# Two cross-attention layers on one core: a packed image product, maxima taken after the second scores, a split last entry and another order of the opening

## The chip, the core and the metric

The kernel runs on one core of a Trainium2 chip. The core has a matrix engine (TensorE, PE in the profile; PEld is its loading of weights), a vector engine (VectorE, DVE), a scalar engine (ScalarE, ACT), GpSimd (POOL) and SyncE (SP), which here only issues transfers. All of them run at once and wait for each other by semaphores. PE writes its products to PSUM, eight banks of 128 x 512 fp32; data that stay on the core lie in SBUF.

The metric is the time of one execution in microseconds of the device, from its start to its end. The profile is one further execution, whose instructions were recorded.

## What is computed

There are 16 batch entries of 256 positions and 320 channels, 20 heads of 16 channels, and a context of 256 tokens of 512 channels for each entry. In layer 1 the first 77 tokens are text and the other 179 image tokens; in layer 2 the first 252 are text and the last four are image tokens. Both layers have this form (shown for layer 2; layer 1 takes its own similarity from one softmax over the channels of all heads together, and has no norms):

```python
q = heads(x @ W_q); k_t = heads(text @ W_k); v_t = heads(text @ W_v)
probs_t = softmax(q @ k_t.T * scale)
text_out = probs_t @ v_t
k_ip = heads(ip @ W_k_ip); v_ip = heads(ip @ W_v_ip)
qsem = l2norm(probs_t @ text)
sem = qsem @ l2norm(ip).T
probs_ip = softmax(q @ k_ip.T * scale + 0.5 * sem) * spatial_mask
out = (text_out + probs_ip @ v_ip) @ W_out + b_out + x
```

The second layer's `x` is the first layer's `out`. All inputs and outputs are fp32.

## The kernel before

**Precision.** A product of two fp32 tiles takes two records of PE in the profile. Most products are therefore made of halves: each tile is split into a rounded part and a remainder (`halves`, lines L187 and L188), both of type fp32r, and `prod` (L260) sums three single-pass products, high by high, high by low and low by high. The same is done in the output projection (`project`, L632). The image product of layer 2 (L1108) is one of those left in plain fp32.

**Slots.** The heads are handled in groups of four, five groups for each entry, so a layer has 80 slots (one slot is one group of one entry): 0 to 79 are layer 1, 80 to 159 layer 2. The queries and keys of a slot, its stacks, are loaded from DRAM four slots ahead (`LEAD`).

**A slot of layer 2** (`slot1`). `both1(k, t)`, once for each half t of the positions, writes the transposed scores of slot k (L917, tiles T, read by ACT's exponential L929) and the plain scores of slot k+2 (L922, tile S). S takes two banks and has a single buffer; T has two tiles, P one and X three of a bank each. DVE takes the maximum over S (L923) and copies the image scores out of it (L939). The maxima are then turned by two products with a unit matrix (`maxima1`, L955) into one row, copied by ACT (L957) and stored by a DMA on ACT's queue (L959) into row `XROW` of the query stack. There it is one more row of the contraction of L917, so that the exponentials are taken of scores less their maximum. `attend1` (L988, L990) multiplies the probabilities by the values into the lower half of a P bank; its last products, with the matrix `zone` (L990), add the sums for the norm, taken from the tiles W. `norm1` multiplies the rounded probabilities (`rounded1`: ACT rounds at L965, POOL keeps the remainder at L966) by a matrix of the context (L975, 14 products of 512 columns in a slot); DVE multiplies the result by W (L978) and the two parts are added (L980, on POOL for the first two heads and on DVE for the others). `settle1` (L1040 to L1044) turns the attended tile with a DVE transpose and divides by the sums.

**An entry of layer 2.** Beside its five slots an entry has steps spread over the slots around it: `k1` its keys (`keys1`; L564 is the remainder of the split), `t1` its values and the context matrix (`tokens1`, L585 to L602), `o1` its queries (`open1`, L615 to L618 and L640, L641), `gather` (L864, three DVE transposes of the result), `i1` the softmax over the image tokens (`image_softmax`, L1051 to L1101, most of it on POOL) and `c1` its end (`close1`): for each of three blocks of rows the image product (L1108, the table `vb` of image values, 128x384, by the turned probabilities `pT`, turned at L1100), the sum with the transposed text result (L1109, on DVE), the split (L871, L873), 24 products with the output weights and the residual (L895). The table of each entry is loaded from `spread_d` in DRAM, which `weights8` makes once at the layer change: it fills it with zeros from a tile and then copies blocks of the image values (`vipd`, stored by `weights6`) to their places.

**What sets the order.** PE's order is written by the program in all stages. In `begin`, which is the opening up to slot 0, every engine's order is; in layer 2 (slots 80 to 159) that of all engines but SP; in layer 1 and after slot 159 the other engines' order is left to the scheduler. Steps are `task`s with due times in slots (the table `STEPS`; for an entry of layer 2 relative to its first slot): at given points of each slot `fill` runs all steps that have come due. DVE instructions that are given to `late` are put off while `hold` is in force and are issued at `release`, or at the next `settled`. Nearly all DMAs are issued by SP, in order, so one that waits holds up those behind it.

**The opening.** `begin` loads the weights and the contexts of entries 0 and 1, makes keys, queries and layer 1's own similarity, and scores slots 0 and 1. The row of maxima of these two slots is stored by SP's queue (L783, behind ACT's copy L782), and the contexts of entries 2 and 3 are loaded behind that.

**The end.** The last entry, b = 15, is closed like the others, behind slots 160 and 161, which only finish the sums of slots 158 and 159.

## Time and profile before

| | us |
|---|---|
| median of 3 runs | 1479.34 |
| lowest and highest | 1478.5, 1482.8 |
| the profiled execution | 1478.29 |
| its span in the profile | 1476.5 |

The mean granted clock of PE in the profiled execution was 0.992 of full speed. The span is the time between the first and the last instruction recorded; the profiled execution's own time is 1.8 us longer.

Rows of the profile read like this: a window has its start and end, then for each engine the busy time and, in parentheses, the instructions counted, then PE's granted clock, the busy share of the DMA engines and the GB/s that they moved. A row of the timeline has the start of a group of equal instructions, the time from there to its last end, the engine, the line of the program, the operation, and output and input tiles with their sizes; in brackets the idle time before it and what ended that. A row of the chain has the start, the length and the engine with its tile and line; "issue" is time in which an engine waited for nothing that the profile shows, SPq a DMA's issue on SP, "DMA x<-y" a transfer.

### The profile page before, as it was taken

What the parts mean: (1) busy time and instruction counts of PE and PEld (TensorE: products, weight loads), DVE (VectorE), ACT (ScalarE), POOL (GpSimd) and SP (SyncE); (2) the same over time, 40 slices, a digit from 0 to 9 for tenths busy, and PEclk for the clock granted to TensorE, in tenths of its full rate; (3) what the DMA queues carried; (4) which work ended last, traced back from release to release, by engine and by line L of the source; (5) the groups of instructions that cost most, each with busy time, mean ns of one, the idle gap of its engine ahead of it and who ended that gap; (6) DMA issues with size and microseconds to landing.
All of it is one profiled execution on the core that took longest, in us unless ns stands there. A gap on an engine that the chain in (4) does not pass through costs nothing.

```text
span 1476.5 us, 35304 instructions
## 1 busy us (share of the span) xinstructions
PE 1431.7 (97%) x12438; PEld 1184.3 (80%) x12438; DVE 1167.9 (79%) x2569; ACT 955.8 (65%) x2074; POOL 1154.1 (78%) x1173
## 2 busy tenths in 40 slices
PE   6899999999999999899999999999999999999998
PEld 6788888888888878677778888888888888888865
DVE  5477776777767787977888888888888888888897
ACT  5567676767676776756666666656665666566563
POOL 5259797978787878987788878787778877887786
PEclk9899999999999999999999999999999999999999
DMA  6766666565656577665434433543454345434511
GB/s 198 170 171 178 149 158 165 152 167 147 170 151 170 149 187 215 146 184 163 135 107 140 147 117 102 161 146 102 119 161 143 93 130 160 133 100 120 150 31 50
DMA packets 230667, 211.78 MB, mean 143 GB/s; under 512 B 56314, under 2 KB 217116, under 8 KB 230492
## 3 DMA queue, kind: packets, MB, share of 16 engines
q1 hardware_dynamic: 229232, 208.57, 50.5%
q8 instruction: 99, 1.62, 0.5%
q10 hardware_dynamic: 1260, 0.97, 0.2%
q14 instruction: 76, 0.62, 0.1%
HBM read 122.07 MB, written 86.44 MB: 141 GB/s over the span
## 4 chain that ended last, share of the span: by engine, by line
PE 87%; DVE 5%; DMA 2%; ACT 2%; issue 2%; POOL 2%; SPq 1%; DVEq 0%; ACTq 0%; POOLq 0%
PE X L260 22%; PE X L975 17%; PE X L632 11%; PE P L833 7%; PE S L772 6%; PE P L988 5%; PE T L917 5%; PE T L795 5%; PE S L922 3%; PE P L990 2%; PE X L690 1%; PE X L1108 1%; POOL wt L966 1%; PE X L780 1%; SPq L83 1%
## 5 line engine op out<-in xcount | busy, mean ns | idle before, releaser
L801 POOL TENSOR_TENSOR P<-P,rs 128x512 f32<-128x512 f32 x320 | 414.4, 1319 | 142.2 <-ACT P L798 142.0
L975 PE MATMUL X<-ctb,gm 128*128 128x512 f32 x1120 | 292.2, 403 | 0.0
L966 POOL TENSOR_TENSOR wt<-P,ctb 128x512 f32<-128x512 f32 x212 | 268.5, 1295 | 0.0
L923 DVE TENSOR_REDUCE mn<-S 128x4 fp32r<-128x1008 f32 x160 | 192.8, 1205 | 80.3 <-PE S L922 78.5
L975 PEld LDWEIGHTS X<-ctb,gm 128*128 128x128 f32 x1120 | 201.2, 188 | 48.7 <-issue 0.4
L798 ACT ACTIVATE P<-T 128x512 f32<-128x512 f32 x320 | 174.7, 593 | 97.6 <-PE T L795 80.0
L978 DVE TENSOR_TENSOR wt<-X,wt 128x512 f32<-128x512 f32 x240 | 159.3, 680 | 4.0 <-PE X L975 3.4
L929 ACT ACTIVATE P<-T 128x512 f32<-128x512 f32 x212 | 115.0, 597 | 54.4 <-PE T L917 41.8
L980 POOL TENSOR_TENSOR wt<-wt 128x512 f32<-128x512 f32 x80 | 103.6, 1295 | 57.5 <-DVE wt L978 57.5
L774 DVE TENSOR_REDUCE mn<-S 128x4 fp32r<-128x716 f32 x160 | 142.4, 890 | 0.0
L965 ACT ACTIVATE ctb<-P 128x512 fp32r<-128x512 f32 x212 | 122.2, 625 | 30.4 <-PE X L975 29.2
L833 PE MATMUL P<-P,vr 128*32 128x256 f32 x1920 | 123.9, 389 | 0.6 <-DVE sp L693 0.6
L632 PE MATMUL X<-hq,wE 128*128 128x256 f32 x768 | 111.4, 290 | 4.9 <-ACT hq L615 3.6
L260 PE MATMUL X<-cta,wA 128*128 128x252 f32 (+3 forms) x726 | 104.9, 290 | 6.1 <-ACT wA L187 5.3
L632 PEld LDWEIGHTS X<-hq,wE 128*128 128x128 f32 x768 | 102.2, 196 | 7.6 <-ACT hq L615 4.0
L632 PE MATMUL X<-ho,wF 128*128 128x256 f32 x768 | 106.6, 285 | 0.9 <-DVE ho L871 0.6
L260 PEld LDWEIGHTS X<-cta,wA 128*128 128x128 f32 (+1 forms) x726 | 94.8, 191 | 10.2 <-ACT wA L187 5.6
L632 PEld LDWEIGHTS X<-ho,wF 128*128 128x128 f32 x768 | 98.7, 189 | 3.9 <-DVE ho L871 1.0
L844 DVE STREAM_TRANSPOSE nt<-P 128x512 f32<-128x512 f32 x80 | 57.1, 714 | 44.6 <-PE P L833 44.4
L833 PEld LDWEIGHTS P<-P,vr 128*32 128x32 f32 x1920 | 55.4, 111 | 41.4 <-issue 5.5
L773 DVE TENSOR_REDUCE mn<-S 128x4 fp32r<-128x308 f32 x160 | 74.4, 465 | 17.4 <-PE S L772 16.9
L917 PEld LDWEIGHTS T<-qs,ks 49*128 49x128 f32 x640 | 50.3, 184 | 46.5 <-issue 19.9
(223 smaller groups left out, 3319.6 us busy)
## 6 DMA issues: line engine op xcount, KB each, us to landing
qd<-q SPq DMA_DIRECT2D x48, 384.0 KB
kd<-kst SPq DMA_DIRECT2D x66, 256.0 KB
rawc<-in_cT_dram SPq DMA_DIRECT2D x60, 256.0 KB
qs<-qd SPq DMA_DIRECT2D x160, 96.0 KB
ks<-kd SPq DMA_DIRECT2D x160, 96.0 KB
qs<-qd SPq DMA_DIRECT2D x60, 192.0 KB
ks<-kd SPq DMA_DIRECT2D x60, 192.0 KB
qd<-q SPq DMA_DIRECT2D x32, 256.0 KB
```

Source lines behind the costliest of these rows:

```text
L260: last = mm(out, lhs(a, k), rhs(b, k), start=i == 0, stop=i == len(terms) - 1)
L632: mm(pp, w(s, k, slice(m * 128, (m + 1) * 128)), a[:, t], start=i == 0, stop=i == len(terms) - 1)
L774: anchor(nc.vector.tensor_reduce(mn[:, t, 1], sp[:, :, T0:], axis=AX.X, op=ALU.max))
L798: exp = anchor(nc.scalar.activation(pt, st[p], AF.Exp, scale=SCALE))
L801: anchor(nc.gpsimd.tensor_mul(pt, pt, rs[:, t : t + 1].to_broadcast([128, 2, S])))
L833: mm(pv[32 * s : 32 * s + 32, o : o + S], v[:, vt, h : h + 32], P[k, s // 2][:, t, s % 2], start=vt < 2, stop=vt != 1,)
L917: mm(st[u][:, j], c[1][rows, j, lo : lo + 128], c[0][rows, j], start=True, stop=True)
L923: anchor(nc.vector.tensor_reduce(maxes[k + 2][:, t], sp[:, :, :T1], axis=AX.X, op=ALU.max))
L965: nc.scalar.activation(R[k, u][:, t], P[k, u][:, t], AF.Copy, scale=0.5)
L966: anchor(nc.gpsimd.tensor_sub(W[k, u][:, t], P[k, u][:, t], f(R[k, u][:, t])))
L975: mm(yp, gm[:, gb], R[k, u][:, kt], start=i == 0, stop=i == len(blocks[n]) - 1)
L978: nc.vector.tensor_mul(product, yp, w[:, n])
```

## The change

- **Packed image product.** `vb` and `pT` are now of type fp32r. The table holds, in the 96 rows that were zero before, also the remainder of the image values: of every 32 rows 8 are used by two groups of heads, and now three times (high, high, low). The probabilities are packed beside it as high, low, high, so that one single-pass product sums all three terms. Groups 0 and 1, 2 and 3, and 4 share the three blocks, so `pT` is three tiles of 128x256 in place of one. For each entry ACT makes four small copies and three of 128x256, POOL two small subtractions, DVE three transposes in place of one. In `weights6` the image values are split (an ACT copy and a DVE subtraction) and stored with three DMAs. In `weights8` three tiles are set to zero by POOL in place of one, and the 24 copies from `vipd` move 192 pieces of 64 bytes in place of 64.
- **Maxima.** `maxima1(k + 1)` comes right behind the second `both1` of slot k and uses the upper half of the bank of `attend1`. Before, `maxima(k + 2)` came at the end of the slot with a bank of its own. `release` and, behind it, `hold` move behind the second scores, `rounded1(k, 0)` behind the third part of `norm1`, `rounded1(k, 1)` behind the stacks. `settle1` keeps its reciprocals in the lower half of the bank.
- **Split last entry.** The image softmax of entry 15 runs for groups 0 to 3 (`i1a`) and then, with DVE in POOL's place, for group 4 (`i1`). `close_first` does two thirds of the rows and of the output products early; `close_last` does the third row and six products. Residual and text result are added by fp32 products with the unit matrix. For the last slot the remainders of its second pair of heads are made on DVE, and the two parts of the norm are added by four more products with `zone`. The output goes out in three DMAs on two queues.
- **Layer change.** The due times of the weight steps stay; those of the steps of layer 2's entries (`k1`, `t1`, `o1`, `i1`, `c1`) change. The zero fill of `spread_d` is issued later on SP, just before the last stacks of layer 1 that precede `vipd`, since its source tiles come free later; all loads of `wq1` stand behind the stores of `vipd`, where the first stood in front of them before.
- **Opening.** `begin` is written out step by step. The loads of the contexts of entries 2 and 3 are issued behind the loads of the stacks of slot 2, and their keys are spread over the rest of `begin`. The row of maxima of slot 1 goes by ACT's queue. The first half of slot 0's transposed scores is made in `begin`, and `opening` takes the place of slot 0.

The order of PE is the same in both programs from about the third slot of layer 1 to shortly before the end of layer 1.

The core of the diff:

```diff
-        dma(vipd, vip)
+        high = buf("rawc", [128, 512], bufs=2, name="high")[:BI, :CP].bitcast(FR)
+        nc.scalar.copy(high, vip)
+        nc.vector.tensor_sub(vip, vip, f(high))
+        for d, v in zip(range(3), (high, high, vip)):
+            dma(vipd[d].rearrange("n b c -> (n b) c"), v)
...
-    def maxima1(k):
-        mn = maxes[k]
-        mp = bank()
+    def maxima1(k, bank):
         for t in range(2):
-            mm(mp[:4, t * 128 : (t + 1) * 128], mn[:, t], ident_r, start=True, stop=True)
+            mm(bank[:4, S + t * 128 : S + (t + 1) * 128], maxes[k][:, t], ident_r, start=True, stop=True)
         mt = buf("mt", [8, S], FR)[:4]
-        nc.scalar.copy(mt, mp[:4, :S])
+        nc.scalar.copy(mt, bank[:4, S:])
         row = QK[k][0].rearrange("(u p) j t -> u p j t", u=2)[:, XROW]
-        late(lambda: nc.scalar.dma_start(f(row), f(mt)))
+        nc.scalar.dma_start(f(row), f(mt))
...
     def slot1(k):
...
-        yield release
         yield lambda: both1(k, 1)
+        yield lambda: maxima(k + 1, summed)
         if last:
             yield lambda: norm1(last, 0, 0)
         yield 0.2
+        yield release
+        if mine:
+            yield hold
         for parts in summed:
             yield lambda: settle1(*parts)
         if last:
             yield lambda: norm1(last, 0, 1)
-        if mine:
-            yield lambda: rounded1(k, 0)
         yield 0.4
         if last:
             yield lambda: norm1(last, 1, 0)
-        yield 0.6
+        if mine:
+            yield lambda: rounded1(k, 0)
         if last:
             yield lambda: norm1(last, 1, 1)
-        if mine:
-            yield hold
+        yield 0.6
+        yield 0.8
+        yield lambda: stacks(k + LEAD)
         if mine:
             yield lambda: rounded1(k, 1)
-        yield 0.8
-        yield lambda: maxima(k + 2)
-        yield lambda: stacks(k + LEAD)
         yield 1.0
...
-        pT = w1["pT"]
-        late(lambda: nc.vector.transpose(pT, pi.rearrange("p f c -> p (f c)")))
+        for d, x in pieces:
+            (nc.vector.tensor_copy if lo else nc.scalar.copy)(d[:, :, :, :8], x)
+            nc.scalar.copy(d[:, :, :, 16:24], x)
+        yield
+        for d, x in pieces:
+            pool.tensor_sub(d[:, :, :, 8:16], x, f(d[:, :, :, :8]))
+        yield
+        turned = w1["turned"]
+        for i in turns:
+            late(lambda i=i: nc.vector.transpose(turned[i], f(packed[i // 2][:, i % 2]).rearrange("p f c -> p (f c)")))
+        yield
+        settled()
+        for i in turns:
+            nc.scalar.copy(pT[i], turned[i])
         return pT, vb
+    def close_first():
+        hT, (pT, vb) = results["gathered", B - 1, 0], get("i1a")
+        settled()
+        x, hl = load(x1d[B - 1], "xq"), buf("ho", [128, 5, S], FR)
+        def row(p):
+            hp = bank()[:, :S]
+            mm(hp, ident, hT[:, p], start=True, stop=False)
+            mm(hp, vb[:, p * 128 : (p + 1) * 128], pT[p], start=False, stop=True)
+            nc.scalar.copy(hl[:, p], hp)
+            low_half(hl, p, hp)
...
+        for m, pp in enumerate(outs):
+            mm(pp, ident, x[:, m], start=True, stop=False)
+            for s, k, t in [(s, k, t) for k in range(2) for s, t in ((0, k), (0, 3 + k), (1, k))]:
+                mm(pp, wo[1](s, k, slice(m * 128, (m + 1) * 128)), hl[:, t], start=False, stop=False)
+            yield
+    def close_last():
+        row, hl, x, outs = get("c1a")
+        get("i1", B - 1)
+        settled()
+        row(2)
+        yield
+        for m, pp in enumerate(outs):
+            for s in range(2):
+                mm(pp, wo[1](s, 2, slice(m * 128, (m + 1) * 128)), hl[:, 2], start=False, stop=s == 1)
...
+    def opening():
+        yield lambda: turned0(0, 1)
+        yield lambda: score0(2, 0)
+        yield 0.2
+        yield lambda: score0(2, 1)
+        yield lambda: stacks0(4, "QK")
+        yield 0.6
+        yield 1.0
```

227 lines of the change are left out of this document (155 added, 72 removed), and 35 rows, old and new, of the table STEPS.

## The prediction

> **What bounds the kernel now.** I read the page's busy times first, then its chain that ended last, then a table of stages, and last the timelines inside one stage.
>
> ```profile
> span 1476.5 us, 35304 instructions
> PE 1431.7 (97%) x12438; PEld 1184.3 (80%) x12438; DVE 1167.9 (79%) x2569; ACT 955.8 (65%) x2074; POOL 1154.1 (78%) x1173
> ...
> PE 87%; DVE 5%; DMA 2%; ACT 2%; issue 2%; POOL 2%; SPq 1%; DVEq 0%; ACTq 0%; POOLq 0%
> ```
>
> TensorE sets the end: 97% busy and 87% of the chain. So the change pays in two ways: fewer microseconds of products where PE has no gap, and shorter gaps where it has one. The stages tell which is where (span, then busy time and count of PE, weight loads, DVE, ACT, POOL, then clock, DMA share, GB/s):
>
> ```profile
> 55.00:60.00 5.00, 1.80 (x13) 1.24 (x11) 3.97 (x11) 2.68 (x10) 0.40 (x1) 0.91 0.39 83
> 60.00:66.00 6.00, 5.68 (x28) 5.55 (x28) 3.69 (x5) 4.07 (x10) 5.03 (x4) 0.51 0.96 280
> 66.00:71.00 5.00, 1.83 (x10) 1.26 (x8) 4.86 (x5) 1.78 (x5) 2.97 (x3) 0.83 0.54 113
> 71.00:77.00 6.00, 6.00 (x40) 4.10 (x40) 2.46 (x5) 1.29 (x3) 0.33 (x1) 0.57 0.01 3
> 990.00:1039.60 49.60, 49.60 (x420) 40.19 (x419) 42.53 (x90) 30.85 (x68) 39.47 (x44) 1.00 0.44 130
> 1388.00:1438.00 50.00, 47.70 (x370) 35.34 (x368) 45.14 (x93) 29.75 (x64) 37.92 (x43) 1.00 0.21 58
> ```
>
> Rows 1 to 4 are the opening: 22 us with 15.31 of them busy, so 6.7 idle; the clock of rows 2 and 4 costs 5.68 x 0.49 + 6.00 x 0.43 = 5.4 more. Row 5 is one batch entry of layer 2: PE busy for all of it, DVE for 86%. Row 6, the last entries: DVE for 90%.
>
> **Part 1, the packed image product.** In each layer 2 entry three fp32 products of 256 columns become single-pass products; 45 of the 48 change (the last entry's three stand in the tail, part 3). The first two rows are PE's timeline in the steady stage, the third is from the chain near the end:
>
> ```profile
> 992.84 1.02 PE L1108 MATMUL X<-rs,rs 128*128 128x256 f32 x4
> ...
> 1001.91 0.59 PE L1108 MATMUL X<-rs,rs 128*128 128x256 f32 x2
> ...
> 1443.69 1.91 PE X L632 x16
> ```
>
> Two records are one fp32 product. Two more of them lengthen the group by 1.02 - 0.59 = 0.43 us, the price of one product without its end. A single-pass product of 256 columns takes 1.91/16 = 0.12. Each saves 0.31: 0.94 an entry, 14.0 in all, if PE stays the bound.
>
> What is added for it stands on other engines: per entry ACT gets four small copies and three of 128x256, POOL two small subtractions, DVE two more transposes of 128x256. ACT was busy for 30.85 of 49.60 and POOL for 39.47: I take nothing for them, their idle 18.8 and 10.1 hide it; uncovered, ACT's three large copies, some 0.36 each by the copy of part 5, would be 1.1 an entry. DVE's two transposes are 2 x 0.44 (L1100 below), which takes it to about 43.4 of 48.7.
>
> **Part 2, the turns of the maxima.** The maxima's two products (L955) move from the slot's end to just behind its second scores (L922), into the free half of the P bank; the row that they give is wanted by the next slot's L917, in the shortest slot (below) 5.63 - 0.33 - 0.21 = 5.1 us later. Even a DMA as long as the 4.92 us load of part 5 would almost fit there and be late by ACT's work ahead of it; each microsecond of that, in the shortest slot of every entry, would be 15 us. The row has 4 KB, the load 256, and I take nothing. Deferred DVE work is let go behind the second scores, too, and what remains runs at the slot's end, ahead of the next slot's first reduction (L923). This is the point where I expect the gain to go. The same slot of before on both engines (start, busy time, idle before):
>
> ```profile
> 1029.32 0.40 PE L922 MATMUL S<-ks,qs 48*128 48x256 f32 x4
> 1029.65 2.83 PE L975 MATMUL X<-ctb,gm 128*128 128x512 f32 x11
> 1032.32 1.55 PE L260 MATMUL X<-cta,wA 128*128 128x252 f32 x12
> 1033.70 0.86 PE L975 MATMUL X<-ctb,gm 128*128 128x512 f32 x3
> 1034.40 1.92 PE L260 MATMUL X<-wC,cta 128*128 128x320 f32 x12
> 1036.16 0.28 PE L955 MATMUL X<-ident_r,mn 128*4 128x128 f32 x2
> 1036.37 0.51 PE L917 MATMUL T<-qs,ks 49*128 49x256 f32 x4
> 1036.71 0.41 PE L922 MATMUL S<-ks,qs 48*128 48x256 f32 x4
> ```
>
> ```profile
> 1029.77 1.21 DVE L923 TENSOR_REDUCE mn<-S 128x4 fp32r<-128x1008 f32 x1 [0.49 <-PE S L922]
> ...
> 1030.97 0.68 DVE L978 TENSOR_TENSOR wt<-X,wt 128x512 f32<-128x512 f32 x1
> 1031.57 0.44 DVE L1040 STREAM_TRANSPOSE nt<-P 128x256 f32<-128x256 f32 x1
> ...
> 1032.49 1.28 DVE L978 TENSOR_TENSOR wt<-X,wt 128x512 f32<-128x512 f32 x2
> 1033.69 1.09 DVE L864 STREAM_TRANSPOSE hT<-hsn 128x256 f32<-128x256 f32 x3
> 1034.70 0.38 DVE L564 TENSOR_TENSOR kst<-X,kst 128x252 fp32r<-128x252 f32 x1
> 1035.01 0.69 DVE L978 TENSOR_TENSOR X<-X,wt 128x512 f32<-128x512 f32 x1
> 1035.73 0.69 DVE L980 TENSOR_TENSOR wt<-wt,X 128x512 f32<-128x512 f32 x1
> 1036.34 0.44 DVE L1100 STREAM_TRANSPOSE rs<-rs 128x256 f32<-128x256 f32 x1
> 1037.15 1.21 DVE L923 TENSOR_REDUCE mn<-S 128x4 fp32r<-128x1008 f32 x1 [0.38 <-PE S L922]
> ```
>
> The score tile S has one buffer, so the reduction must be over before PE writes the next scores. Before, DVE waits 0.38 to 0.49 us for PE ahead of each reduction shown, and PE never for DVE. In the changed order one slot of each entry holds on PE, from its second L922 to the next slot's first, only 14 of L975 (2.67 + 0.70), 12 of L260 (1.38), L955 (0.21), L917 (0.34) and L922 itself (0.33): 4.93 + 0.70 = 5.63 us. On DVE it holds from reduction to reduction, start to start: L923 with its copy 1.20, L978 0.60, L1040 with the two behind it 0.92, two of L978 1.20, three of L864 1.01, L564 0.31, the last L978 0.72 and L980 0.61: 6.57 us. DVE comes 0.94 late. PE notices this at its second score write, which waits for that reduction; its slack there is 0.38 (by the smaller idle time; a reduction without such slack behind it would cost all 0.94). So 0.56 us of stall, where L922's wait also holds up the L975 products behind it and by them the next L978. Another slot, with L1060, L1109, L873, L587 and L618 packed ahead of the reduction, comes out near its PE time; I take 0.25, between nothing and 0.5. The other three are longer on PE and on time. Together 0.8 an entry against 0.94 saved: net -0.14, over 15 entries -2. Bounds: -14 (no stall) and, with 0.94 and 0.5 lost in full, +7.
>
> [...]
>
> **Part 3, the split last entry.** The rows are from the chain of the tail:
>
> ```profile
> 1453.31 5.08 POOL wt L966 x4
> ...
> 1458.56 1.25 POOL wt L980
> ...
> 1469.17 3.15 PE X L632 x23
> ```
>
> The last slot's POOL subtractions are halved between POOL and DVE, and L980's sum goes to PE as four more zone products: 2.5 + 1.25 us less on POOL, against DVE work that is then itself on the chain, about 4 L978 and two subtractions (0.6 each) in the fullest stage of DVE (45.14 of 50). I keep 0.7. Of the 3.15 us of output products only 6 of 24 stay behind the last row: 2.4 less; three smaller output DMAs on two queues instead of one change little. Sum -3, between -1 (DVE late) and -6.
>
> **Part 4, the layer change.** Weights keep their due times; eight products of the first entry's queries go earlier. What moves on the SP queue is the zero fill of the spread table, four DMAs of 768 KB, and the loads of wq1, which now stand behind the stores of vipd (a line of the DMA table, then SP's queue):
>
> ```profile
> spread_d<-kb SPq DMA_DIRECT2D x4, 768.0 KB
> ```
>
> ```profile
> 603.01 0.36 SPq L83 DMA_DIRECT2D rawc<-in_wq_dram  x1
> ...
> 611.83 0.46 SPq L83 DMA_DIRECT2D vipd<-rawc  x1
> ```
>
> The fill moves to just ahead of the key and query stacks that precede vipd, and waits there for two buffers; 3.1 MB at the 280 GB/s of row 2 above are 11 us of DMA time, queued in front of those stacks and of wq1. The stacks are loaded four slots (30 us) ahead, so I take +1, from -2 (products pulled into gaps) to +6 (half the fill seen).
>
> **Part 5, the opening.** The chain there, and SP's queue:
>
> ```profile
> 57.98 0.36 ACT mt L782
> ...
> 60.50 4.92 DMA raw<-in_cT_dram
> ...
> 67.78 3.10 DVE ctb L188 x2
> ...
> 70.92 0.74 PE X L260 x2
> ```
>
> The context loads of entries 2 and 3 stand on SP behind the row of maxima and are issued only once ACT has made it (57.98 + 0.36). In the change that row goes by ACT's queue and the loads stand behind the third stack's, before the first scores, some 15 us earlier, so the 4.92 us landing and DVE's halves (3.10) come before PE needs them; key products of these entries fill PE. What is late next is DVE: four halves of 1.5 us and the reductions between them. I take half of the 6.7 + 5.4 lost: -6.5, from -2 to -11.
>
> [...]
>
> **The sum**, against the profiled execution: 1478.3 (span 1476.5 and 1.8 around it) - 2 - 3 + 1 - 6.5 = 1467.8. The median of the runs shown, 1479.3, is 1.0 above it, inside their 4.3 of spread: I add nothing and say 1468.
>
> **The rivals.** (A) PE stays the bound in layer 2: the reductions find slack that I don't see. For it: DVE is busy for only 43.4 of 48.7. Against it: the 6.57 against 5.63. Then -14 in place of -2: 1456. (B) My forecast, 1468. (C) The score reduction decides and the kernel becomes slower: DVE, late in one slot, hands its lateness on, since L978 frees the X banks that L975 fills. At 1478.3 + 1 - 3 - 6.5 - 14 = 1455.8 without stalls it takes 28 us, 1.9 per entry, to be above 1483.8, that is twice the lateness worked out; with the fill of part 4 seen at +6, 1.5. It would give some 1488. For it: 0.38 us of slack in a stage where DVE does 86%. Against: three of five slots give DVE time to catch up. (E) In the changed program L1040, which reads the lower half of the P bank, waits for ACT's copy of the maxima out of the upper half. If that copy ended last, each of 80 slots would get its 0.36 us (part 5) on DVE, 29 us: 1497. Against it: L1040 has the reduction (1.20) and an L978 (0.60) between it and the second scores, and ACT is busy for 31 of 50. (D) The opening doesn't do what it says: the loads run earlier, but DVE's halves hold PE up as long as before. Without the 6.5, 1474.3.
>
> **How the numbers follow.** A 0.25, B 0.47, C 0.12, D 0.13, E 0.03. The range 1453 to 1482 takes in A, B and D with their bounds and leaves out C, E and a little under A, where the tail and the opening give all they can. What a measurement of this kernel can tell from no change is 0.3%, 4.4 us: faster is below 1474.9 and slower above 1483.8. A, most of B and half of D are faster: 0.70; the rest of B and D within: 0.15; slower are C and E: 0.15.
>
> **What would show it.** Part 1: each image product a single record of some 0.12 us to the next. Part 2: an entry of the steady stage takes 49.4 to 49.6 us, with PE idle about 0.6 us in front of one L922 per entry, released by DVE's L923; 48.7 without gaps would be A, above 50.5 C. L1040 waiting for ACT in most slots would be E. Part 3: from the last zone products to the end about 3 us less. Part 4: no gap over 3 us between 600 and 640. Part 5: context loads issued near 40 us, the two half-clock stretches gone, and the 130th microsecond's work reached 6.5 earlier. The prediction is wrong if DVE's idle time in front of the first reductions is still there in every slot, or if it is gone in most.

## The result, and the profile after

| | before | after |
|---|---|---|
| median, us (12 runs of each on the same chip) | 1479.28 | 1487.65 |
| lowest and highest | 1477.05, 1484.39 | 1484.47, 1493.14 |
| the profiled execution | 1478.29 | 1484.90 |
| its span | 1476.5 | 1483.1 |

The ratio is 1.0047, 95% interval 1.0034 to 1.006: slower, by 8.4 us in the medians and 6.6 in the two profiles. The forecast was 1468. The page of the changed kernel begins (span, busy times, and from its fourth part the chain's shares):

```profile
span 1483.1 us, 35388 instructions
PE 1422.8 (96%) x12410; PEld 1173.9 (79%) x12410; DVE 1174.6 (79%) x2607; ACT 969.1 (65%) x2187; POOL 1161.1 (78%) x1197
...
PE 78%; DVE 7%; DMA 6%; issue 3%; POOL 2%; ACT 2%; SPq 1%; ACTq 0%; DVEq 0%; POOLq 0%
```

PE is busy for 8.9 us less (1431.7 before) and the span is 6.6 longer: its idle time rose from 44.8 to 60.3 us. On the chain its share fell from 87 to 78%, and DVE (5 to 7) and DMA (2 to 6) took the place. The products became cheaper; the waits became dearer.

Where it happened is read from a mark that both programs have in every slot, the start of the slot's first maximum on DVE (L774 and L923 before, L787 and L937 after). The next table says how much a stage took more (+) or less than in the profile of before. Layer 2 begins with slot 80; slot 95 is the first of its fourth entry, 155 the first of its last. The forecast stands in the last column.

| stage | before, us | changed kernel | forecast |
|---|---|---|---|
| start to slot 10 | 131.53 | -6.0 | -6.5 |
| slot 10 to 70 | 460.02 | 0.0 | 0 |
| slot 70 to 95, the layer change and the first entries | 207.69 | +14.4 | +1 |
| slot 95 to 155, twelve entries | 596.58 | -6.9 | -1.7 |
| slot 155 to 159 | 34.90 | +0.1 | |
| slot 159 to the end | 45.79 | +5.1 | -3 |

Two stages decide: the layer change, forecast at 1, cost 14.4, and the end lost 5.1 where 3 were to be gained. These are single profiles: in the versions below that share the stage's program the layer change came out between 14 and 19, the end (slot 159 on) between +3.8 and +5.5, and the opening between -3.5 and -7. A difference of a few us between two profiles of such a stage is therefore no finding by itself.

The windows that answer to those of before, in the same columns:

```profile
49.00:54.00 5.00, 1.94 (x19) 1.75 (x17) 1.63 (x3) 1.78 (x4) 0.00 (x0) 0.90 0.71 227
54.00:60.00 6.00, 4.76 (x23) 4.79 (x24) 2.64 (x5) 3.04 (x6) 2.52 (x2) 0.51 0.80 224
...
990.00:1039.10 49.10, 48.78 (x417) 39.48 (x416) 43.02 (x92) 31.61 (x75) 40.31 (x46) 1.00 0.44 131
```

The first two rows are of the opening: where before had two half-clock stretches (0.51 and 0.57), one is left, 54 to 60. The last is a steady entry, half a microsecond shorter than before but with 0.32 idle.

The two stages that lost, each as one window, from mark to mark; first before (two views), then the changed kernel:

```profile
591.55:799.24 207.69, 196.27 (x1753) 156.34 (x1756) 171.47 (x359) 134.48 (x288) 173.02 (x172) 0.99 0.52 149
```

```profile
1430.72:1476.50 45.78, 38.38 (x274) 27.39 (x274) 35.08 (x84) 17.73 (x41) 30.23 (x43) 0.99 0.16 48
```

```profile
585.49:807.55 222.06, 199.98 (x1741) 158.09 (x1744) 173.50 (x359) 132.58 (x289) 173.98 (x174) 0.97 0.55 155
...
1432.19:1483.10 50.91, 41.57 (x288) 28.88 (x287) 38.37 (x99) 23.34 (x63) 29.36 (x40) 0.97 0.14 43
```

Span less busy time of PE is its idle time. At the layer change it went from 11.4 to 22.1 us, 10.7 more, and busy time rose by 3.7 though 12 fewer products were recorded: the clock, 0.97 in place of 0.99. At the end idle time went from 7.4 to 9.3, and busy time rose by 3.2, in part by 14 more products, in part by the clock.

**The opening** (SP's queue, then PE's timeline):

```profile
40.80 0.90 SPq L84 DMA_DIRECT2D rawc<-in_cT_dram  x2
41.75 1.59 SPq L84 DMA_DIRECT2D raw<-in_cT_dram  x2
```

```profile
55.24 1.19 PE L808 MATMUL T<-qs,ks 127*128 127x256 f32 x4 [4.30 <-DMA qs<-mt]
```

The context loads are issued at 40.8, against 59.1 before. What remains is one wait of 4.30 us, for the row of maxima, and with it the half clock of window 54 to 60 (0.51). From the start to slot 10 PE's idle time fell by only 1.5 us (19.5 to 18.0); its busy time fell by 4.5 (112.1 to 107.6) with one product more recorded, at a mean granted clock of 0.96 in place of 0.92. So most of the gain is clock.

**The layer change** (chain of waits, then PE's timeline):

```profile
597.85 9.62 DMA qs<-qd
...
656.14 5.10 DMA qd<-q
...
661.65 2.36 DMA qs<-qd
```

```profile
607.61 0.71 PE L785 MATMUL S<-ks,qs 125*128 125x256 f32 x4 [2.11 <-DMA qs<-qd]
...
663.45 0.38 PE L936 MATMUL S<-ks,qs 48*128 48x256 f32 x1 [2.38 <-DMA qs<-qd]
```

There are two waits for query stacks. The first load took 9.62 us behind the zero fill. The second stack could only be loaded behind the store of the first entry's queries (5.10), and this store came late (SP's queue of the changed kernel, then the store in that of before):

```profile
592.64 3.77 SPq L84 DMA_DIRECT2D spread_d<-kb  x4
...
654.86 3.05 SPq L84 DMA_DIRECT2D qd<-q  x3
```

```profile
647.20 2.03 SPq L83 DMA_DIRECT2D qd<-q  x3
```

What such a gap can cost beyond itself is seen in the windows around the second, and around one of 1.48 us at 767:

```profile
661.00:663.40 2.40, 0.07 (x2) 0.00 (x0) 0.44 (x2) 0.66 (x3) 0.02 (x1) 1.00 0.49 145
663.40:665.00 1.60, 1.33 (x5) 0.91 (x6) 0.12 (x1) 0.00 (x0) 0.00 (x0) 0.69 0.69 213
665.00:667.00 2.00, 2.00 (x10) 2.00 (x11) 1.17 (x2) 0.64 (x2) 0.00 (x0) 0.50 0.73 198
667.00:669.00 2.00, 2.00 (x28) 1.08 (x26) 0.48 (x1) 0.45 (x1) 1.96 (x2) 0.89 0.44 116
767.00:769.00 2.00, 0.52 (x8) 0.33 (x4) 1.50 (x3) 1.83 (x4) 2.00 (x3) 1.00 0.00 0
769.00:771.00 2.00, 2.00 (x13) 1.63 (x10) 1.50 (x3) 0.36 (x1) 2.00 (x3) 0.71 0.13 24
771.00:773.00 2.00, 2.00 (x11) 2.00 (x11) 0.48 (x1) 0.00 (x0) 1.16 (x1) 0.50 0.56 183
773.00:775.00 2.00, 2.00 (x11) 1.65 (x10) 1.07 (x4) 1.73 (x5) 0.52 (x1) 0.94 0.00 0
```

Busy time by the share of the clock that is missing: 1.33 x 0.31 + 2.00 x 0.50 + 2.00 x 0.11 = 1.6 us in the first case, 0.58 + 1.00 + 0.12 = 1.7 in the second.

**The steady entries** (PE's timeline; then its groups from 850 to 1350, with count, busy us, mean ns, and the idle time before them):

```profile
995.01 0.50 PE L936 MATMUL S<-ks,qs 48*128 48x256 f32 x4 [0.25 <-DVE sr L953]
...
1000.61 0.40 PE L1190 MATMUL X<-kb,tph 128*128 128x256 f32 x2
...
1091.35 0.50 PE L931 MATMUL T<-qs,ks 49*128 49x256 f32 x4 [1.50 <-DMA qs<-mt]
```

```profile
L931 PE MATMUL T<-qs,ks 49*128 49x256 f32 x408 | 54.7, 333 | 2.7 <-DMA qs<-mt 2.2
...
L936 PE MATMUL S<-ks,qs 48*128 48x256 f32 x408 | 42.9, 286 | 2.0 <-DVE sr L953 2.0
...
L1190 PE MATMUL X<-kb,tph 128*128 128x256 f32 x22 | 4.4, 280 | 0.0
```

Two image products take 0.40 us and one takes 0.28: a further one costs 0.12, as forecast. PE waits for DVE ahead of second scores, as forecast, though less: 2.0 us in ten entries. It also waits 2.2 us, in two places, for the row of the maxima, a wait that I had priced at nothing; its worst case is the 1.50 above.

**The end** (DVE's timeline, then PE's):

```profile
1436.04 1.09 DVE L877 STREAM_TRANSPOSE hT<-hsn 128x256 f32<-128x256 f32 x3
1437.13 0.77 DVE L1136 STREAM_TRANSPOSE rs<-kb 128x256 f32<-128x256 f32 x2
1437.83 0.40 DVE L1136 STREAM_TRANSPOSE rs<-tph 128x256 f32<-128x256 f32 x1
...
1439.19 1.28 DVE L991 TENSOR_TENSOR wt<-X,wt 128x512 f32<-128x512 f32 x2
```

```profile
1441.28 1.30 PE L1005 MATMUL P<-wt,zone 128*32 128x256 f32 x8 [2.20 <-POOL wt L993]
```

Six deferred transposes go ahead of the products for the norm sums, and PE stands 2.20 us in front of the zone products. The releaser named is POOL's L993; it adds what DVE's L991 of 1439.19 made, so it is late by the transposes, too.

### The profile page after: what moved, and what is told of

The parts are those of the page before. It is cut to its first block, busy times and chain, and to the rows that moved or that the text cites. A ratio compares the mean times of both kernels' runs of the same rounds, so it can differ in the third digit from the quotient of the medians.

```text
span 1483.1 us, 35388 instructions
## 1 busy us (share of the span) xinstructions
PE 1422.8 (96%) x12410; PEld 1173.9 (79%) x12410; DVE 1174.6 (79%) x2607; ACT 969.1 (65%) x2187; POOL 1161.1 (78%) x1197
## 4 chain that ended last, share of the span: by engine, by line
PE 78%; DVE 7%; DMA 6%; issue 3%; POOL 2%; ACT 2%; SPq 1%; ACTq 0%; DVEq 0%; POOLq 0%
PE X L261 20%; PE X L988 15%; PE X L645 11%; PE P L846 6%; PE S L785 5%; PE T L808 4%; PE P L1001 4%; PE T L931 3%; PE S L936 3%; DMA kd<-kst 2%; PE P L1005 2%; DVE mn L937 2%; SPq L84 1%; POOL P L814 1%; PE X L703 1%
## 5 line engine op out<-in xcount | busy, mean ns | idle before, releaser
L988 PE MATMUL X<-ctb,gm 128*128 128x512 f32 x1120 | 287.1, 399 | 1.4 <-DVE hsn L1069 0.6
L937 DVE TENSOR_REDUCE mn<-S 128x4 fp32r<-128x1008 f32 x160 | 192.4, 1202 | 65.0 <-PE S L936 64.5
L991 DVE TENSOR_TENSOR wt<-X,wt 128x512 f32<-128x512 f32 x241 | 162.4, 686 | 13.2 <-PE X L988 9.8
L993 POOL TENSOR_TENSOR wt<-wt 128x512 f32<-128x512 f32 x79 | 102.4, 1296 | 54.3 <-DVE wt L991 41.4
L787 DVE TENSOR_REDUCE mn<-S 128x4 fp32r<-128x716 f32 x160 | 142.4, 890 | 0.0
L645 PE MATMUL X<-hq,wE 128*128 128x256 f32 x768 | 106.6, 286 | 4.4 <-ACT hq L628 3.7
L645 PE MATMUL X<-ho,wF 128*128 128x256 f32 x744 | 102.6, 284 | 0.1
```

The lines of the kernel that those rows point to most:

```text
L645: mm(pp, w(s, k, slice(m * 128, (m + 1) * 128)), a[:, t], start=i == 0, stop=i == len(terms) - 1)
L787: anchor(nc.vector.tensor_reduce(mn[:, t, 1], sp[:, :, T0:], axis=AX.X, op=ALU.max))
L937: anchor(nc.vector.tensor_reduce(maxes[k + 2][:, t], sp[:, :, :T1], axis=AX.X, op=ALU.max))
L988: mm(yp, gm[:, gb], R[k, u][:, kt], start=i == 0, stop=i == len(blocks[n]) - 1)
L991: nc.vector.tensor_mul(product, yp, w[:, n])
```

## The experiments

"After" is the changed kernel, and every edit is made in it. Each measurement gives the median in us and the ratio to the kernel before, run on the same chip, with its 95% interval; since the kernel before has medians from 1478.57 to 1484.04 on the chips of these runs, versions are compared by these ratios (after: 1.0047) and by stages.

### The steady entries: what the three parts are worth

Part 1 alone taken back, the image product in plain fp32 (its preparation is still made; the same edit is made in `close_first`):

```diff
-            mm(hp, bd[:, p * 128 : (p + 1) * 128], pT[p], start=True, stop=True)
+            mm(hp, f(bd[:, p * 128 : (p + 1) * 128]), f(pT[p]), start=True, stop=True)
```

> The changed kernel with the packed image product read as plain fp32 (two records instead of one), all packing kept: it gives back only the matmul time. If PE sets the pace of layer 2's entries: 0.31 us for each of three products, an entry of slots 100 to 155 goes from 49.1 to 50.0 us, the time up by 12 to 15. If the late score reductions set it, as predicted: an entry stays within 0.3 us of 49.1 and the time within 4.

Measured: 1506.02, ratio 1.0165 (1.0128 to 1.0203). An entry takes 50.40 us (mean of slots 100 to 150), against 49.16 in after and 49.69 before. In the groups of PE, 850 to 1350:

```profile
L931 PE MATMUL T<-qs,ks 49*128 49x256 f32 x400 | 53.3, 333 | 4.6 <-DMA qs<-mt 4.2
```

PE pays for the products, so they are on the path; beyond the 0.94 of the products themselves the waits for the row grow by 0.2 an entry.

Part 2 alone taken back, the turn order of before in `slot1` (maxima in a bank of their own, their store put off as before):

```diff
+        yield release
         yield lambda: both1(k, 1)
-        yield lambda: maxima(k + 1, summed)
...
-        yield release
-        if mine:
-            yield hold
...
+        yield lambda: maxima(k + 2)
         yield lambda: stacks(k + LEAD)
```

> The changed kernel with the slot of before: maxima at the slot's end in a bank of their own, release ahead of the second scores, hold behind norm1, rounded1 at the old places. Theory 1, the new turns cost more than they bring: PE's gaps in front of one score write per entry (0.23 us in the middle of the layer, 0.7 in its first entries) go, an entry comes to 48.7 to 48.9 us instead of 49.1, the 2.2 us gap in slot 159 goes, time 1474 to 1481. Theory 2, they are neutral or help: entries of 49.1 or longer, time 1486 to 1492.

Measured: 1509.92, ratio 1.02 (1.0153 to 1.0248); an entry takes 50.29. So the new turn order, of which I expected a loss, is worth 1.1 us an entry beside the packed product, with the due times as they are in the changed kernel; the old order with due times of its own was not run. The two together are not a sum. With both taken back (`split_only` and `no_split`, below) an entry takes 50.59 and 50.49, with either alone 50.40 or 50.29, and with both 49.16. And `no_split`, whose steady entries differ from those of before in the main by the preparation of the packed tables and by due times, is 0.8 an entry slower than before. Its groups say where:

```profile
L936 PE MATMUL S<-ks,qs 48*128 48x256 f32 x392 | 41.8, 283 | 5.5 <-DVE sr L953 5.5
```

PE waits 0.55 an entry for DVE ahead of second scores, which it did not in these entries before (0.0 us ahead of L922). The two added transposes put 0.88 us more on DVE; that they are the cause, and not a due time, fits and was not tried alone.

The lateness of DVE alone: the three transposes of `gather` (L877), which stand ahead of a first reduction, go behind it.

```diff
-            late(lambda p=p: nc.vector.transpose(hT[:, p], ...))
+            make = lambda p=p: nc.vector.transpose(hT[:, p], ...)
+            turned.append(make) if b < B - 2 else late(make)
...
         yield lambda: both1(k, 0)
+        while turned:
+            turned.pop(0)()
```

> The changed kernel with the three transposes of each entry's text result (L877, 1.0 us of DVE) issued behind the first score reduction of the next slot instead of ahead of it. Theory 1, late reductions hold PE: the gaps of 0.79 us before a score write in entries 1 to 3 and of 0.23 in later entries go, slots 85 to 95 lose at most 3 against before (4.6 to 5 in the changed kernel and its variants) and an entry comes to 48.8 to 48.9 us instead of 49.1; time 1482 to 1485. Theory 2: the reductions behind come late by the same amount: no change, 1486 to 1489.

Measured: 1478.76, ratio 1.0001 (0.998 to 1.0022), 0.46% below after; an entry takes 48.61. DVE's timeline, and PE's groups:

```profile
1089.13 1.21 DVE L938 TENSOR_REDUCE mn<-S 128x4 fp32r<-128x1008 f32 x1 [0.34 <-PE S L937]
...
1090.34 1.09 DVE L877 STREAM_TRANSPOSE hT<-hsn 128x256 f32<-128x256 f32 x3
```

```profile
L932 PE MATMUL T<-qs,ks 49*128 49x256 f32 x408 | 55.0, 333 | 1.2 <-DMA qs<-mt 0.5
```

DVE waits for PE ahead of the reduction again, no group of second scores waits for DVE any more, and the maxima come in time for most of the waits on their row to go, too (2.2 to 0.5). From slot 95 to 155 that is -13.4 us, against -6.9 in after. The lateness was real, and this one move takes 0.55 off an entry. PE's idle time between 850 and 1350 accounts for 0.35 of it (4.8 us of 500 in after, 1.2 here); the other 0.2 is in PE's busy time and stays unexplained.

### The layer change

The zero fill back to its old place on SP, by exchanging two allocations:

```diff
-        packed, zero = [buf("kb"
+        zero, packed = [buf("kb"
```

> One name swapped: the zero fill of spread_d takes its zeros from the buffer that comes free first, as before the change; nothing else differs, and only SP's order moves (the fill about 35 us earlier, ahead of nothing that is waited for). Theory 1, the fill in front of the stacks of layer 1's last slots is what the layer change loses: from the first score reduction of slot 70 to that of slot 95 the changed kernel takes 14.4 us more than before; here it takes 5 to 9 more, the load of the query stack lands in about 3 us instead of 9.6, and the time is 1479 to 1482. Theory 2, SP's queue is slowed by the 24 longer copies of vipd and the later loads of wq1, and the fill does nothing: that stretch still takes 13 to 15 more, time 1486 to 1488.

Measured: 1487.51, ratio 1.0034 (1.0018 to 1.005); slot 70 to 95 +17.8. The 9.62 us load is gone, and PE's wait for it, and the time stays: 17.8 lies among the 14 to 19 of unchanged versions. This was the mechanism on which I had put +6 as a bound: undoing it gives nothing that these runs show.

The fill early, and a buffer of its own for the rounded image values (`high`):

```diff
-        high = buf("rawc", [128, 512], bufs=2, name="high")[:BI, :CP].bitcast(FR)
+        high = const_tile([BI, CP], "high", FR)
```

> The changed kernel with the early zero fill and a buffer of its own for the rounded image values, so that the loads of wq1 need not wait until the stores of vipd have read a load buffer. Theory 1, that wait is the first part of the loss: from slot 72 to slot 75 the changed kernel and its early fill take 6 us more than before; here at most 2 more, with the first load of wq1 issued before the stores as in before, and the time 3 to 5 below the early fill's 1487.5. Theory 2, DVE and ACT are full in these slots (DVE 9.5 of 10) with the split of the image values and the halves of wq1, whenever these land: 4 to 6 more, time within 2 of 1487.

Measured: 1486.84, ratio 1.0015 (0.999 to 1.0039); slot 70 to 95 +16.7. Against `fill_early` no gain clear of the noise, either in the time or in the stage.

The due times of keys, tokens and queries (`k1`, `t1`, `o1`) of entries 0 and 1 set back to those of before, six lines of `STEPS`, of which the first and last are:

```diff
-        ("k1", 0): (-7.8, -6.2, -6.2, -5.2, -4.2, -3.2,),
+        ("k1", 0): (-7, -6.2, -5.8, -5, -4.6, -3,),
...
-        ("o1", 1): (-6.6, -6.6, -5.6, -5.6, -4, -3.8,),
+        ("o1", 1): (-6.8, -6.8, -6.2, -5.8, -4, -3.8,),
```

> The changed kernel with the due times of before for keys, values and queries of the first two entries of layer 2 (k1, t1, o1 of entries 0 and 1). Theory 1, these times are what the layer change loses: from slot 70 to slot 95, 14 to 18 us longer than before in the changed kernel and the runs so far, here at most 8 longer; time 1478 to 1482. Theory 2, the loss comes from the layer change's own additions (three stores of vipd, longer copies, wq1 behind them) and from late DVE work in slots 85 to 95: 12 or more, time 1485 to 1489.

Measured: 1489.61, ratio 1.0027 (1.0004 to 1.005); slot 70 to 95 +17.5. No gain. Then one of the six lines alone, the queries of entry 0:

```diff
-        ("o1", 0): (-7.2, -7, -6.6, -5.2, -3.6, -3.6,),
+        ("o1", 0): (-7, -7, -5.6, -5.2, -4, -4,),
```

> The changed kernel with one row of due times put back, that of the first entry's queries (o1 of entry 0): its last eight products come before slot 76's scores instead of behind them. Theory 1: in the changed kernel they come at 649.3 us, their store is issued at 656.1 and the query stack lands for slot 80's scores only at 664, with 2.4 us of PE gap and half clock behind it. Put back, that gap goes and the stretch from slot 77's to slot 81's first score reduction, 6.6 us longer than before in the changed kernel, is at most 3 longer; time 1481 to 1485. Theory 2, SP's queue is late there whatever the products do, because of the copies of vipd: the stretch stays 5 to 7 longer, time 1486 to 1489.

Measured: 1484.27, ratio 0.9993 (0.9971 to 1.0015), 0.54% below after. The store of the queries goes out 2.2 us earlier, though slot 77 stands 4.8 us later in this profile than in that of after (SP's queue):

```profile
652.68 1.83 SPq L84 DMA_DIRECT2D qd<-q  x3
```

From slot 77 to 81 it takes +2.1 where after takes +6.6, and the gap at 661 with its half clock is gone (granted clock 1.00 from 655 to 675). This is outside what single profiles do: the three versions below that also have this line take +1.9 to +2.2 there, all versions of the changed kernel without it +5.8 to +9.6. Of the entry's six query steps the change pulls two forward and puts the last two, due at -4, to -3.6. The six were put back together; that it was the last two that made the store late is argued from their place ahead of it. The prediction had only seen products that go earlier. In `due01`, which has this line too, PE does not wait for the query stack between slots 77 and 81 either; it waits 2.24 us for ACT (at 643) and 1.56 for POOL (at 673) instead, which it does in neither after nor `o1_old`. So another of the six lines takes the gain away; which one was not run.

Part of what else is lost between slot 77 and 95 is DVE's lateness, in the first entries worse (0.79 us ahead of a second score) than in the steady ones (0.25 at 995), I take it since PE has no closing products of layer 2 to do there (the first L1190 starts at 804.5); no run shows that it is this. Of the changed kernel, DVE's timeline and PE's:

```profile
746.03 0.69 DVE L993 TENSOR_TENSOR wt<-wt,X 128x512 f32<-128x512 f32 x1
746.64 1.09 DVE L877 STREAM_TRANSPOSE hT<-hsn 128x256 f32<-128x256 f32 x3
...
747.96 1.19 DVE L937 TENSOR_REDUCE mn<-S 128x4 fp32r<-128x1008 f32 x1
```

```profile
749.38 0.50 PE L936 MATMUL S<-ks,qs 48*128 48x256 f32 x4 [0.79 <-DVE sr L953]
```

These 0.79 us, 0.79 at 739 and the 1.48 at 767 (with its half clock) are such waits, but only the first stands behind the three transposes. Ahead of the late reduction at 738 DVE splits a weight (L189, 2.20 us), ahead of that at 767 it makes a step of a later entry's queries (L631, 1.44). With the transposes moved (`late_turns`) slot 81 to 95 takes +2.9 in place of +4.8 here and 5 to 9 in the other versions with the new turn order that leave them in place; the waits of 0.79 and 1.49 stay. So some 2 us of the 4.8 are the transposes', and the other 2.9 no run took away; nor did any take away the 3 us from slot 70 to 77.

### The end

The last entry closed as before, in one piece:

```diff
-ENDED = 2 * NS - 1
+ENDED = 2 * NS
...
-        ("c1", B - 1): (7.2, 7.8,),
+        ("c1", B - 1): (12.2, 13, 13, 13.2, 13.4, 16,),
...
-        if b < B - 1:
+        if True:
             task(("c1", b), at("c1", b), lambda b=b: close1(b)
...
-    task(("c1a",), [2 * NS + t for t in STEPS["c1a"]], close_first, ("i1a",), ("c1", B - 2))
-    task(("c1", B - 1), at("c1", B - 1), close_last, ("c1a",), ("i1", B - 1))
```

> The changed kernel with the end of before: entry 15 closed like the others, the last slot's remainders on POOL, the parts of the norm added by POOL and DVE. Theory 1, the new end loads DVE where it is full: from slot 159's first score reduction to the end the changed kernel takes 50.9 us and before 45.8; here 45.5 to 47, time 1482 to 1484. Theory 2, the loss comes from the deferred DVE work that the new place of release puts ahead of slot 159's products (a PE gap of 2.2 us and half clock behind it), which this run keeps: 49 us or more, time 1486 to 1489.

Measured: 1494.11, ratio 1.0064 (1.0034 to 1.0094). From the last zone products to the end it takes 19.7 us, with the split 14.2, before 15.9. Against before that is 1.7 us, of the 3 that I had expected there; against the unsplit end with the packed path, 5.5. The loss stands ahead of the last zone products: slot 159's mark to their end takes 29.9 us before and 36.7 after.

Three edits move the norm sums ahead of the deferred transposes. The first, of slot 159, where there was no such wait, was aimed at the wrong slot:

```diff
         yield 0.2
+        if k == 2 * NS - 1:
+            yield lambda: norm1(last, 0, 1)
         yield release
```

> The changed kernel, in slot 159 alone the second part of norm1 ahead of release, so that its DVE product runs before the six deferred transposes. Theory 1: the 2.2 us that PE waits for POOL's sum in slot 159, and the half clock behind it, are what the new end loses: from slot 159's first score reduction to the last zone product the changed kernel takes 36.7 us and before 29.9; here 32 to 33.5, the end 3 to 5 earlier, time 1483 to 1485. Theory 2: the deferred work is only moved and holds up the next zone product instead: 36 or more, time 1487.

Measured: 1489.84, ratio 1.0037 (1.0013 to 1.0062); the gap of 2.2 us, which lies in slot 157, stayed. The second moved one sum of slot 157:

```diff
             yield lambda: norm1(last, 0, 0)
+        if k == 2 * NS - 3:
+            yield lambda: norm1(last, 0, 1)
```

> The edit of the run before at the slot where it belongs: scores are two slots ahead, so the 2.2 us gap stands in slot 157, not 159. There the second part of norm1 comes ahead of the first point at which deferred work is issued, so its DVE product precedes the six transposes. Theory 1: the gap before the zone products (2.2 us, for POOL's sum) and the half clock behind it are the larger part of the new end's loss. From slot 159's first score reduction to the last zone product the changed kernel takes 36.7 us and before 29.9: here 32 to 34, time 1483 to 1485. Theory 2: the work is only moved and the next products wait for it: 36 or more, time 1487.

Measured: 1491.48, ratio 1.0074 (1.0051 to 1.0097); one zone product (two records of eight) went early, and the next waited 3.26 us for the others' sum. The third moved all four:

```diff
             yield lambda: norm1(last, 0, 0)
+        if k == 2 * NS - 3:
+            yield lambda: norm1(last, 0, 1)
+            yield lambda: norm1(last, 1, 0)
+            yield lambda: norm1(last, 1, 1)
         yield 0.2
         yield release
```

> The changed kernel with all four norm sums of the last entry's first combination issued in its slot ahead of the deferred transposes, so that VectorE makes them first. Theory 1 (the tail is late because the turns of the maxima put three to six transposes ahead of these sums, and the first zone products wait for them): the gap of 2.2 us ahead of the zone products is under 1 us, no half clock in the stretch 1440 to 1450, the time from the last slot's first reduction to the end falls from 50.9 us by 2.5 to 4.5, and the kernel takes 1482 to 1485. Theory 2 (VectorE is full there, so the transposes made later hold up something else): 50 us or more in that stretch and 1486 to 1490.

Measured: 1489.03, ratio 1.0049 (1.0026 to 1.0071), 51.3 us from slot 159 to the end. The gap ahead of the zone products is gone, and PE stands elsewhere (its timeline):

```profile
1442.78 1.07 PE L1001 MATMUL P<-P,v1t 128*32 128x256 f32 x16 [1.14 <-DVE wt L993]
...
1445.73 2.17 PE L988 MATMUL X<-ctb,gm 128*128 128x512 f32 x7 [0.80 <-ACT ctb L977]
...
1452.34 0.38 PE L645 MATMUL X<-ho,wF 128*128 128x256 f32 x1 [1.23 <-ACT ho L894]
```

Theory 2: the delay moved. What was late by the transposes is now on time, and what stood behind it waits for DVE and ACT in turn.

Last, is it the split, or the packed product and the turns at work in these slots? `split_only` has plain product and old turn order (the two diffs above), with the split; `no_split` has the same with the last entry closed in one piece. Both unsplit versions keep the other edits of the end: the last group's image softmax on DVE, the last text result gathered in two parts, and the rewritten slots 160 and 161.

> The changed kernel with both the plain fp32 image product and the old order of the second turn: of the three changes of layer 2 the split last entry alone remains (with the opening and the layer change). Time from the last slot's first reduction to the end, 45.8 us before and 50.9 in the changed kernel. Theory 1 (the packed product and the new turn order made the tail late, the split is worth what was predicted): 42 to 45 us. Theory 2 (the split itself puts work and waits in front of the end): 48 to 52 us. Whole time by either: 1495 to 1510.

> As split_only, with the last entry unsplit too: layer 2 is that of before but for the opening, the layer change, and the copies for the packed product, which are still made. The same stretch of time: by theory 1 3 to 6 us longer than in split_only; by theory 2 45 to 47 us, 3 to 6 us shorter than in split_only.

Measured: 1516.21, ratio 1.0234 (1.0177 to 1.029), and 1515.91, ratio 1.0208 (1.0151 to 1.0266). From slot 159's mark to the end:

| | unsplit | split |
|---|---|---|
| before | 45.8 | |
| plain product, old turns, tables packed | 57.0 | 54.8 |
| packed product, new turns | 55.5 | 50.9 |

The 54.8 is above both ranges that were expected for `split_only`, so its number alone decides nothing; the table does, as far as single profiles go (that of `split_only`, 1526.0, was 9 us or more above its three other runs). The split gains 2.2 to 4.6, in both rows: theory 2 falls. Theory 1 falls in its first half, since the end is late without the packed product and the new turns, too. What costs is in what `no_split` has beside the kernel before: the preparation of the packed tables, the due times of the last entries' softmax and closing (entry 14's closing begins 0.8 of a slot later), and the other edits just named. Together they lose 11.2 us, of which 4.2 are waits for ACT's copies of the packed tables, with the clock behind them (PE's timeline, then a window):

```profile
1501.29 2.08 PE L1192 MATMUL X<-kb,tph 128*128 128x256 f32 x4 [2.86 <-ACT kb L1142]
1504.66 1.22 PE L1192 MATMUL X<-tph,tph 128*128 128x256 f32 x2 [1.30 <-ACT tph L1142]
```

```profile
1494.30:1515.30 21.00, 12.64 (x66) 10.14 (x61) 10.66 (x36) 4.10 (x14) 2.50 (x7) 0.73 0.19 64
```

In the steady entries other products stand between the softmax and the image product, and PE waits 0.0 us ahead of it (L1192, 850 to 1350); in the last entry no such products are left. `old_tail` waits 3.54 and 1.88 us for the same copies; before waits 1.03 us at this place, for a transpose of DVE, so 3.1 of the 4.2 are new. By the window's mean clock some 12.64 x 0.27 = 3.4 us more are the clock. The other 4.7, and with them how much the due times of entry 14 or the other edits take, no run told apart.

### Versions put together

The opening of the change alone, in the kernel before:

> The kernel of before with nothing but the new opening (its order of steps and the due times of the first entries of layer 1). If the opening is worth what the changed kernel shows at slot 10 and keeps until slot 70, 6.0 us, and nothing behind it depends on it: 1473 to 1475 on a chip on which before takes 1479 to 1480. If the layer change or the end takes it back: 1477 or more.

Measured: 1475.66, ratio 0.9977 (0.9958 to 0.9996), 2.9 us below before; its profiled execution, 1486.0, was slower than all its others (1472.8 to 1477) and is not read here. Then the diffs of `o1_old`, `norm157` and `late_turns` in one kernel:

> The changed kernel with three edits together: the first entry's queries at their old due times, norm1 first in slot 157, the late transposes. If the three losses are separate, their gains add up: 3.5 from the first, 3 from the second, 3 from the third, 1477 to 1480; if each only moves a wait to the next engine, 1483 or more.

Measured: 1475.87, ratio 0.9967 (0.9947 to 0.9988). Without that of `norm157`, and with the transposes of entry 14 moved, too (`b < B - 1`):

> The changed kernel with the old due time of the last query products and with the half-batch transposes of every entry but the last behind the next slot's first reduction, nothing else. If the two edits add (3.4 and 8.9 us when made alone): 1474 to 1477. If the transposes of entry 14 are also among those that made the tail late: 1472 to 1474.

Measured: 1475.37, ratio 0.9951 (0.9934 to 0.9968). And with the diff of `norm_all`:

> combo3 with the four norm sums ahead of the deferred transposes as well. Theory 1 (the sums are late because of the transposes): 2.5 to 4.5 us below combo3, 1469 to 1473. Theory 2 (only moved): within 1 us of combo3.

Measured: 1476.4, ratio 0.9953 (0.993 to 0.9975), no difference to `combo3`: theory 2 again. `combo3` is faster than both kernels, 0.5% below before and 1% below after. Its stages add up to the end of its span: -5.7 up to slot 70, +10.9 to slot 95, -13.4 to slot 155, +0.1 to slot 159, +5.2 to the end, together -2.9.

## Why the prediction was wrong, step by step

**The bound.** Right: PE sets the pace in the steady stage, and the products taken away there show (with the 0.94 us of `plain_product` put back an entry takes 1.24 more). That DVE's lateness takes part of it back was right, too.

**Part 1, the packed product.** Products: right, 0.12 us each, and by `plain_product` the 0.94 an entry is on the path. "I take nothing" for the preparation did not hold: in the old turn order an entry with it, and with the new due times, is 0.8 longer (`no_split` against before), and 0.55 of this is PE waiting for DVE. The two transposes were counted as load, and not asked which reduction they precede.

**Part 2, the turns.** The mechanism and the place were right: DVE behind, PE waiting at the second score write (0.25 us at 995), released by the copy behind L937, in the slot with three L877. Its size was not: 0.8 an entry forecast, 0.55 measured (after against `late_turns`), which holds the waits on the row, priced at nothing. Between slots 95 and 155 the net came to -0.58 an entry instead of -0.14: the stalls were 0.25 smaller, and without them an entry is 1.1, not 0.94, below before. The range given for this term, -14 to +7, held it. `late_turns` is what rival A described, PE without gaps, and more: -13.4 in twelve entries, where A's -14 in fifteen is -11.2 in twelve. That C's 1488 is the time that came is luck: its 1.5 to 1.9 us of lateness an entry did not come about. E fell (groups of DVE in the changed kernel, the last number being idle time); a wait of its kind is in `norm_all`, 1.91 us in the last slots (DVE's timeline):

```profile
L1065 DVE STREAM_TRANSPOSE nt<-P 128x256 f32<-128x256 f32 x80 | 35.1, 438 | 0.0
```

```profile
1449.92 0.45 DVE L1069 STREAM_TRANSPOSE nt<-P 128x256 f32<-128x256 f32 x1 [1.91 <-ACT mt L969]
```

**Part 3, the end.** The smaller of the two steps that failed is "45 of the 48 change (the last entry's three stand in the tail, part 3)": part 3 then priced the split, and not the packed path that the last entry also takes. The split's own term, -3 with bounds -6 and -1, was right (-2.2 to -4.6). What the packed path, the due times and the order around it cost took this away and 5.1 us more; the forecast had bounded "DVE late" at -1, that is, without a loss. How the loss divides among them stays open beyond the waits for ACT's copies.

**Part 4, the layer change.** The step that failed most: +1 forecast, bounds -2 and +6, 14.4 measured. The fill, to which the bound belonged, gives nothing when undone. That "eight products of the first entry's queries go earlier" passed over the two steps that go 0.4 of a slot later: with the line put back, 4.5 us less between slots 77 and 81. The steady stage's stall was not carried into the first entries: some 2 us there are the transposes'. And no price was put on the clock, though the opening had shown one: this stage has four half-clock stretches, where before has one, and three more at the 1.6 to 1.7 us worked out above are some 5 of the 14.4. This cuts across the parts named by slots and does not add to them. The rest of the 14.4, the 3 us up to slot 77 among it, stays open.

**Part 5, the opening.** The path was right, the loads 18 us earlier, and -6.0 came for -6.5; in part that is luck. Half of 6.7 + 5.4 is 6.05 and not 6.5, and the gain did not come half from idle time: idle fell by 1.5, and the clock gave most of the rest. Of "the two half-clock stretches gone" one is left, with a wait for the row of maxima; the same opening gave between 3.5 and 7 in the other profiles, and by `open_only` 2.9 in the medians (0.6 to 6.2 by its interval). The remaining stretch goes with the gap of 4.30 us: the granted clock is 0.50 from 53.0, inside that gap, to 59.7. In the opening of before the longest idle times ahead of its 0.51 and 0.57 were shorter, 1.57 and 2.02 us.

**The sum.** With the measured terms it is 1478.3 - 6.1 + 14.4 - 6.9 + 0.1 + 5.1 = 1484.9, the profiled execution's own time. The forecast's terms erred by +0.4 (opening), +13.4 (layer change), -4.9 (entries) and +8.1 (end); with the +0.1 these are the 17.1 by which it missed.

## What to carry to other kernels

Work that goes to engines with idle time is not free (0.8 us an entry in `no_split`): ask of each added instruction what stands behind it in its queue, and in the last entry, where nothing else runs, add its whole latency. Read every due time that goes later before those that go earlier: one line of query steps, two of them put off by 0.4 of a slot ahead of a store and a load, cost 4.5 us, where taking a 3.1 MB fill away from in front of a stack gained nothing. And where PE is nearly always busy (48.78 of 49.10 us), look for what can go behind the instruction that PE waits for: three transposes moved there gave 6.5 us in twelve entries.

## What the runs showed that I had not expected

Half the clock behind short gaps, but not behind each. In the changed kernel idle times of 1.48 us (at 767), 2.11 (605), 2.20 (1439) and 2.38 (661) were each followed, 0.6 to 1.8 us after their end, by 3.4 us at a granted clock of 0.50 (769.8 to 773.2, 609.4 to 612.8, 1442.3 to 1445.7, 664.0 to 667.4), which cost up to 1.7 us more; those of 1.46 (623), 1.50 (619), 1.50 (1090) and 1.92 (516) were followed by the full clock. A gap of 1.24 us was followed by half the clock in `combo3` (at 685) and not in the changed kernel (at 687), and the gap of 1.48 at 767 was, with 1.49 us at 770, not followed by it in `late_turns`. So length alone does not decide: a gap of 1.2 to 2.4 us was followed by up to 1.7 us of lost clock or by none.

Gains that are far from a sum. An entry takes 50.49 us with the tables packed alone, 50.29 with the packed product, 50.40 with the new turn order, 49.16 with both. Part of it is seen in PE's waits between 850 and 1350: the old order leaves 5.5 us for DVE ahead of the second scores, the plain product 4.2 us for the row, where both together leave 2.0 and 2.2. The rest is not explained.
